# Shaping DMA transfers by their outermost size: eight-part loads and stores, uneven pieces, and a first result laid out by channel

## The chip, the cores and the metric

One core of a Trainium2 chip runs the whole program. The metric is the device time of one execution in microseconds (us). Runs of one kernel agree within about 1.2%; all timed runs quoted with a ratio were in the fast state. "Stages" below are read from one traced execution of each kernel: the **first stage** ends where the first `spread` matmul starts, **layer one** where the second set of them starts, **layer two** is the rest.

## The reference, cut to what matters

Two layers of the same form. Each normalises x over groups (32 groups along the last axis, statistics per sample over the other two axes), makes convolution weights for every position from a small network, and convolves:

```python
# x: (32, 32, 64, 256) = sample s, image b, channel c, position l, float32
w   = (relu(ln(z @ W1 + b1)) @ W2 + b2).reshape(B, L, CI, CO, 3)    # other weights at every position
out = einsum('sbilk,bliok->sbol', windows_of_3(gn(x)), w) + bias    # bias (B, CO, L) from another small net
x   = x + out                                                      # layer 0, then the same for layer 1
```

A "half sample" below is one image b and half its output channels, the unit `v` of the kernel's loop: 64 in each layer.

## The kernel before

The first stage loads all of x (64 MB) for statistics while it makes the hidden values and the bias, which it writes to DRAM (`hd`, `bd`). Then, for each half sample, TensorE makes the weights (`make`, into `pg`) and applies those of the previous half sample (`products`, into `pc`); DVE and ACT place the weights, DVE adds the products to the residual, GpSimd normalises x and adds the bias to the residual. All big transfers are issued on SP's queue.

```python
# layout in DRAM of x for statistics and residual, of x for layer one, of the first result, of the bias
xs: (128 = quarter of positions x sample, half sample, 32, 64)     xp: (image, 2, 128 = parity x channel, 16, 128)
x1 = [dram.tile([S, C, L], FP, name=f"x1_{b}") for b in range(B)]
bd = [dram.tile([2, NT, C, LT], FP, name=f"bd_{i}") for i in range(U // 2)]

def load_pairs(u, k):                      # x that is normalised
    t = pairs(u, k)
    if u < B:
        nc.sync.dma_start(out=t, in_=xp[u, k])
    else:
        src = x1[u - B][k * SH : (k + 1) * SH].rearrange("s c l -> c s l")
        nc.sync.dma_start(out=t[0:C], in_=src)
        nc.sync.dma_start(out=t[C:P, :, 0 : L - 1], in_=src[:, :, 1:L])

def load(q):                               # first statistics, 4 MB each, three in flight
    nc.sync.dma_start(out=xv[q % NX], in_=xs[:, q * SV : (q + 1) * SV])

def load_bias(v):                          # the same bias for all 32 samples
    ...
    for t in range(NT):
        src = bd[u // 2][u % 2, t, h * CH : (h + 1) * CH, :]
        nc.sync.dma_start(
            out=bts[v][t * S : (t + 1) * S],
            in_=bass.AP(src.tensor, src.offset, [[0, S]] + list(src.ap)),
        )
# ... (cut: normalisation, weights, products, stores)
```

Of the kernel before, what the change touches and what calls it, by code (L numbers as in the profile page):

```python
# [23 lines left out]
FP = mybir.dt.float32  # L24
# [6 lines left out]
P = 128  # L31
K = 3
G = 32
NT = 4
NH = 2
OG = 8
EPS = 1e-5
PARAMS = ("z", "W1", "b1", "g1", "be1", "W2", "b2", "Wb1", "bb1", "gb1", "beb1", "Wb2", "bb2")

# [2 lines left out]
def conv_layers(ctx: ExitStack, tc: tile.TileContext, xs: bass.AP, xp: bass.AP, layers: list, out: bass.AP):  # L42


    nc = tc.nc
    B, _, _, SH, M = xp.shape
    S, C, L = 2 * SH, P // 2, 2 * M
    A = layers[0]["z"].shape[0]
    E = L // G
    LT = L // NT  # L50
    MT = M // NT
    CH = C // NH
    EB = 512 // CH
    NB = LT // EB
    GT = G // NT
    F = 4 * CH
    WT = CH + MT * F + CH
    NL = len(layers)
    U = NL * B
    SV = 4  # L60
# [9 lines left out]
    dram = ctx.enter_context(tc.tile_pool(name="dram", bufs=1, space=DRAM))  # L70
    ps_g = ctx.enter_context(tc.tile_pool(name="ps_g", bufs=3, space=PSUM))
    ps_c = ctx.enter_context(tc.tile_pool(name="ps_c", bufs=2, space=PSUM))

    x1 = [dram.tile([S, C, L], FP, name=f"x1_{b}") for b in range(B)]
    hd = [dram.tile([2, P, L], FP, name=f"hd_{i}") for i in range(U // 2)]
    bd = [dram.tile([2, NT, C, LT], FP, name=f"bd_{i}") for i in range(U // 2)]

    w2 = big.tile([P, C, K * C], FP, name="w2t")

# [7 lines left out]
    rstd = const.tile([P, G, S], FP, name="rstd")  # L87
    parts = const.tile([P, GT, B, NH, 6], FP, name="parts")
    prep = const.tile([P, 3, GT], FP, name="prep")
    ident = const.tile([P, P], FP, name="ident")  # L90
# [3 lines left out]
    eps = const.tile([P, 1], FP, name="eps")  # L94
    nc.vector.memset(eps, EPS)

# [8 lines left out]
    for n, par in enumerate(layers):  # L105
        t = const.tile([P, K, C], FP, name=f"b2_{n}")
# [18 lines left out]
    def load_pairs(u, k):  # L125
        t = pairs(u, k)
        if u < B:
            nc.sync.dma_start(out=t, in_=xp[u, k])
        else:
            src = x1[u - B][k * SH : (k + 1) * SH].rearrange("s c l -> c s l")  # L130
            nc.sync.dma_start(out=t[0:C], in_=src)
            nc.sync.dma_start(out=t[C:P, :, 0 : L - 1], in_=src[:, :, 1:L])

    def residual(v):
        return ys[:, v % RING]

    def load_residual(v):
        u, h = divmod(v, NH)
        if u < B:
            nc.sync.dma_start(out=residual(v), in_=xs[:, v])  # L140
        else:
            for t in range(NT):
                nc.sync.dma_start(
                    out=residual(v)[t * S : (t + 1) * S],
                    in_=x1[u - B][:, h * CH : (h + 1) * CH, t * LT : (t + 1) * LT],
                )


# [20 lines left out]
    class Hidden:  # L169
# [54 lines left out]
        def bias(self):  # L224
            p3 = ps_c.tile([C, BLK], FP, tag="pc", name="p3")
            nc.tensor.matmul(p3, self.t["Wb2"], self.ht[:, 1, :], start=True, stop=True)  # L226
            bs = self.stage.tile([C, 2, M, 2], FP, tag="bs", name="bs", bufs=2)
            nc.scalar.activation(
                bs.rearrange("o b m a -> o b a m"),
                p3.rearrange("o (b a m) -> o b a m", b=2, a=2),  # L230
                AF.Identity,
                bias=self.t["bb2"],
            )
            nc.scalar.dma_start(
                out=bd[self.i].rearrange("b t o l -> o (b t) l"),
                in_=bs.rearrange("o b (t m) a -> o (b t) (m a)", t=NT),
            )



    def first_stats():

        NC = NH * B
        with tc.tile_pool(name="stage", bufs=1) as stage:
            spare = stage.tile([P, SV * CH * LT], FP, name="spare")
            flat = [xn.rearrange("p b m s -> p (b m s)"), spare, room]
            xv = [r[:, 0 : SV * CH * LT].rearrange("p (v o l) -> p v o l", v=SV, l=LT) for r in flat]
            NX = len(xv)

            def load(q):  # L250
                nc.sync.dma_start(out=xv[q % NX], in_=xs[:, q * SV : (q + 1) * SV])

            for q in range(NX):
                load(q)
                if q == 0:
                    small = [small_weights(stage, par, n) for n, par in enumerate(layers)]
            zts = []
            for j in range(2):
                zts.append(stage.tile([A + 1, ZB * BLK], FP, name=f"zt_{j}"))
                nc.vector.memset(zts[j], 1.0)  # L260

            made = {0: Hidden(stage, zts, small, 0)}

            def step(s, half):

                if half == 0:
                    if s in made:
                        made[s].project()
                    if s - 2 in made:
                        made.pop(s - 2).bias()  # L270
                    if s in made:
                        made[s].root()
                else:
                    if s - 1 in made:
                        made[s - 1].scale()
                    if s + 1 < U // 2:
                        made[s + 1] = Hidden(stage, zts, small, s + 1)

            n = NC * GT
            when = {k * n // (U + 4): k for k in range(U + 4)}  # L280
            for i in range(n):
                if i in when:
                    step(*divmod(when[i], 2))
                v, g = divmod(i, GT)
                u, h = divmod(v, NH)
                q, j = divmod(v, SV)
                nc.vector.bn_stats(parts[:, g, u, h, :], xv[q % NX][:, j, :, g * E : (g + 1) * E])  # L287
                if j == SV - 1 and g == GT - 1:
                    if q + NX < NC // SV:
                        load(q + NX)  # L290
                    if q + NX == NC // SV - 1:
                        for o0 in range(0, C, 2 * OG):
                            load_w2(0, o0, o0 + 2 * OG)
                    if q % NX == 2 and q + NX >= NC // SV:

                        for k in range(2):
                            load_pairs(0, k)
                        for v in range(2):
                            load_residual(v)

    def stats():

        st = parts.rearrange("p g b h (two f) -> p g (b h two) f", two=2)
        n = st.shape[2]
        shape = [P, GT, n]
        m, v, d = prep[:, 0], prep[:, 1], prep[:, 2]
# [25 lines left out]
    with tc.manual_schedule():  # L332
# [14 lines left out]
        bts = {}  # L347

        def load_bias(v):
            u, h = divmod(v, NH)  # L350
            bts[v] = bp.tile([P, CH, LT], FP, tag="bt", name="bt")
            for t in range(NT):
                src = bd[u // 2][u % 2, t, h * CH : (h + 1) * CH, :]
                nc.sync.dma_start(
                    out=bts[v][t * S : (t + 1) * S],
                    in_=bass.AP(src.tensor, src.offset, [[0, S]] + list(src.ap)),
                )

        def add_bias(v):
            y = residual(v)  # L360
# [2 lines left out]
        def store(v):  # L363
            u, h = divmod(v, NH)
            if u < B:
                for t in range(NT):
                    nc.sync.dma_start(
                        out=x1[u][:, h * CH : (h + 1) * CH, t * LT : (t + 1) * LT],
                        in_=residual(v)[t * S : (t + 1) * S],
                    )  # L370
            else:
                nc.sync.dma_start(out=out[:, v - NH * B], in_=residual(v))

        def normalize(u, k):
            ss = slice(k * SH, (k + 1) * SH)
# [7 lines left out]
        def make(h, kind, o0):  # L383
            pg = ps_g.tile([P, OG, M], FP, tag="pg", name="pg")
            even, odd = h[:, 0, :], h[:, 1, :]

            (k0, h0), (k1, h1) = (((1, even), (2, even)), ((0, odd), (1, odd)), ((2, odd), (0, even)))[kind]
            for k in range(OG):
                w = w2[:, o0 + k, :]
# [4 lines left out]
        def take(pg, n, kind, o0):  # L394

            def place(rows, a):
                a += o0 % CH
                return at(wall[rows, 0, a : a + 1], [[WT, NT], [F, MT], [1, OG]])

            def add(rows, a):  # L400
                nc.vector.tensor_tensor(  # L401
                    place(rows, a),
                    pg[rows].rearrange("p o (t m) -> p t m o", t=NT),
                    b2[n][rows, kind, None, None, o0 : o0 + OG].to_broadcast(
                        [rows.stop - rows.start, NT, MT, OG]
# [88 lines left out]
        for v in range(NH * U):  # L494
            u, h = divmod(v, NH)
# [32 lines left out]


def _orders(x):  # L530


    import numpy as np

    s, b, c, l = x.shape
    xs = x.reshape(s, b, NH, c // NH, NT, l // NT).transpose(4, 0, 1, 2, 3, 5)
    xp = x.reshape(2, s // 2, b, c, l // 2, 2).transpose(2, 0, 5, 3, 1, 4)
    return {
        "xs": np.ascontiguousarray(xs).reshape(P, b * NH, c // NH, l // NT),
        "xp": np.ascontiguousarray(xp).reshape(b, 2, P, s // 2, l // 2),  # L540
    }


# [23 lines left out]
def _result(y):  # L567
    import numpy as np

    y = y.reshape(NT, P // NT, -1, 64, y.shape[-1])  # L570
    return np.ascontiguousarray(y.transpose(1, 2, 3, 0, 4)).reshape(*y.shape[1:4], -1)


# [7 lines left out]
```

## Time and profile before

| kernel before | us |
|---|---|
| median of 4 runs | 4610.9 (4603.3 to 4617.2) |
| first stage, in the trace | 289.1 |
| layer one, in the trace | 2049.7 |
| layer two, in the trace | 2253.7 |

How to read it: the prediction works out that matmuls alone need 1928 us per layer, and that nearly all of the rest is "issue", time in which TensorE stands still and waits for nothing that the profile shows. The first stage is another matter: it is close to bound by the DMA engines. Its line in the busy times by stretch (start and end, length, then busy time of each engine with its count of instructions, granted clock, DMA share, GB/s):

```profile
200.00:250.00 50.00, 46.63 (x125) 28.02 (x124) 41.93 (x115) 22.56 (x35) 24.08 (x49) 0.57 0.85 309
```

The reader is to keep the last two numbers: DMA busy 0.85 of the time at 309 GB/s.

### The profile page before, as it was taken

What the parts mean: (1) busy time and instruction counts of PE and PEld (TensorE: products, weight loads), DVE (VectorE), ACT (ScalarE), POOL (GpSimd) and SP (SyncE); (2) the same over time, 40 slices, a digit from 0 to 9 for tenths busy, and PEclk for the clock granted to TensorE, in tenths of its full rate; (3) what the DMA queues carried; (4) which work ended last, traced back from release to release, by engine and by line L of the source; (5) the groups of instructions that cost most, each with busy time, mean ns of one, the idle gap of its engine ahead of it and who ended that gap; (6) DMA issues with size and microseconds to landing.
All of it is one profiled execution on the core that took longest, in us unless ns stands there. A gap on an engine that the chain in (4) does not pass through costs nothing.

```text
span 4592.5 us, 193878 instructions
## 1 busy us (share of the span) xinstructions
PE 4069.4 (89%) x90704; PEld 3883.6 (85%) x90704; DVE 2642.2 (58%) x3168; ACT 1291.2 (28%) x4264; POOL 2074.9 (45%) x618
## 2 busy tenths in 40 slices
PE   6889999999999999999969888888888888888888
PEld 3569999999999988899868888888888888888888
DVE  6876666666666666666645454545444554454455
ACT  3432232332322322223222222222222222222222
POOL 3465544455444554445344353353443533534532
PEclk9689999999999999999989999999999999999999
DMA  8874444445444454444567667576576675765764
GB/s 307 330 239 133 142 142 133 133 133 148 146 142 124 124 150 142 130 126 133 160 162 165 143 151 170 134 166 152 134 173 141 153 169 134 168 157 137 174 148 107
DMA packets 760621, 718.23 MB, mean 156 GB/s; under 512 B 567492, under 2 KB 715016, under 8 KB 716296
## 3 DMA queue, kind: packets, MB, share of 16 engines
q1 hardware_dynamic: 724488, 683.80, 56.5%
q10 hardware_dynamic: 35328, 22.03, 1.7%
q8 instruction: 709, 11.62, 1.1%
q14 instruction: 96, 0.79, 0.1%
HBM read 558.93 MB, written 146.80 MB: 154 GB/s over the span
## 4 chain that ended last, share of the span: by engine, by line
PE 82%; issue 9%; DVE 3%; DMA 3%; POOL 2%; ACT 1%; ACTq 0%; SPq 0%; POOLq 0%; DVEq 0%
PE pg L390 48%; PE pc L433 23%; PE pg L391 10%; DVE wall L401 2%; POOL sq L198 1%; DMA bd<-bs 1%; PE p L186 1%; DMA zt<-in_L_conv_z_dram 1%; DVE parts L445 1%; DVE room L442 1%; DMA room<-x 1%; PE p L226 0%; ACT ht L216 0%; ACT sq L190 0%; PE p L213 0%
## 5 line engine op out<-in xcount | busy, mean ns | idle before, releaser
L391 PE MATMUL pg<-hT,w2t 128*64 128x128 f32 x24576 | 2808.4, 278 | 60.7 <-issue 60.6
L390 PE MATMUL pg<-hT,w2t 128*64 128x128 f32 x24576 | 2808.6, 278 | 56.5 <-issue 48.2
L390 PEld LDWEIGHTS pg<-hT,w2t 128*64 128x64 f32 x24576 | 2758.8, 140 | 82.3 <-issue 61.9
L391 PEld LDWEIGHTS pg<-hT,w2t 128*64 128x64 f32 x24576 | 2759.2, 140 | 60.7 <-issue 60.7
L401 DVE TENSOR_TENSOR wall<-pg,b 128x1024 f32<-128x1024 f32 (+1 forms) x1536 | 1869.0, 1220 | 870.7 <-PE pg L391 866.8
L416 ACT ACTIVATE wall<-pg,b 64x128 f32<-64x128 f32 x4096 | 1176.7, 481 | 3090.3 <-DVE wall L401 2224.6
L380 POOL TENSOR_TENSOR xn<-room,gmean 128x2048 f32<-128x2048 f32 x128 | 606.6, 4739 | 2205.5 <-DMA room<-x 1104.4
L433 PE MATMUL pc<-wall,xn 128*32 128x128 f32 (+2 forms) x40960 | 1047.4, 261 | 313.3 <-issue 288.9
L433 PEld LDWEIGHTS pc<-wall,xn 128*32 128x32 f32 x40960 | 988.9, 114 | 379.1 <-issue 351.9
L442 DVE TENSOR_TENSOR room<-pc,room 128x512 f32<-128x512 f32 x512 | 354.1, 692 | 1002.4 <-PE pc L433 883.7
L380 POOL TENSOR_TENSOR xn<-xn,rstd 128x2048 f32<-128x2048 f32 x128 | 782.5, 6113 | 10.0
L361 POOL TENSOR_TENSOR room<-room,bt 128x2048 f32<-128x2048 f32 x128 | 593.4, 4636 | 82.3 <-DMA bt<-bd 72.3
L445 DVE BATCH_NORM_STATS2 parts<-room 128x6 f32<-128x256 f32 x512 | 192.9, 418 | 8.7
L198 POOL TENSOR_TENSOR sq<-sq 128x512 f32<-128x512 f32 (+2 forms) x192 | 103.6, 540 | 156.1 <-ACT sq L190 143.6
L186 PE MATMUL p<-wc,zt 17*128 17x256 f32 x256 | 99.8, 553 | 39.3 <-DMA zt<-in_L_conv_z_dram 39.3
L186 PEld LDWEIGHTS p<-wc,zt 17*128 17x128 f32 x256 | 67.5, 277 | 63.1 <-issue 39.7
L213 PEld LDWEIGHTS p<-ident,hs 128*128 128x128 f32 x256 | 50.2, 223 | 49.9 <-issue 49.9
L226 PE MATMUL p<-ht,Wb 128*64 128x512 f32 x64 | 56.7, 985 | 20.5 <-ACT ht L216 20.2
L213 PE MATMUL p<-ident,hs 128*128 128x128 f32 x256 | 62.7, 426 | 3.7 <-DVE hs L204 3.7
L287 DVE BATCH_NORM_STATS2 parts<-xn 128x6 f32<-128x256 f32 x192 | 64.0, 409 | 0.0
L287 DVE BATCH_NORM_STATS2 parts<-spare 128x6 f32<-128x256 f32 x160 | 53.5, 412 | 0.0
L287 DVE BATCH_NORM_STATS2 parts<-room 128x6 f32<-128x256 f32 x160 | 53.5, 412 | 0.0
(44 smaller groups left out, 231.4 us busy)
## 6 DMA issues: line engine op xcount, KB each, us to landing
bt<-bd SPq DMA_DIRECT2D x512, 256.0 KB, 8.9
room<-in_xp_dram SPq DMA_DIRECT2D x64, 1024.0 KB, 8.2
room<-in_xs_dram SPq DMA_DIRECT2D x64, 1024.0 KB, 6.4
x<-room SPq DMA_DIRECT2D x256, 256.0 KB, 4.2
room<-x SPq DMA_DIRECT2D x64, 1024.0 KB, 9.2
room<-x SPq DMA_DIRECT2D x256, 256.0 KB, 5.4
out_dram<-room SPq DMA_DIRECT2D x64, 1024.0 KB, 5.9
room<-x SPq DMA_DIRECT2D x64, 1020.0 KB, 12.9
```

The costliest lines, as they stand in the source:

```text
L186: nc.tensor.matmul(self.p1[:, k], self.zt[:, k * P : (k + 1) * P], self.t["wc"], start=True, stop=True)
L198: nc.gpsimd.tensor_tensor(to, self.sq[:, :, 0:w], self.sq[:, :, w : 2 * w], ALU.add)
L287: nc.vector.bn_stats(parts[:, g, u, h, :], xv[q % NX][:, j, :, g * E : (g + 1) * E])
L361: nc.gpsimd.tensor_tensor(y, y, bts.pop(v), ALU.add)
L380: nc.gpsimd.tensor_tensor(o, i, b, op)
L390: nc.tensor.matmul(pg[0:C, k, :], w[:, k0 * C : (k0 + 1) * C], h0, start=True, stop=True)
L391: nc.tensor.matmul(pg[C:P, k, :], w[:, k1 * C : (k1 + 1) * C], h1, start=True, stop=True)
L401: nc.vector.tensor_tensor(place(rows, a), pg[rows].rearrange("p o (t m) -> p t m o", t=NT), b2[n][rows, kind, None, None, o0 : o0 + OG].to ...
L416: nc.scalar.activation(place(rows, 0)[:, :, :, k], pg[rows, k].rearrange("p (t m) -> p t m", t=NT), AF.Identity, bias=b2[n][rows, kind, o0 ...
L433: nc.tensor.matmul(pc[t * S : (t + 1) * S, n0 - q * EB : n1 - q * EB, :], xn[:, u % 2, t * MT + p + 1, :], wall[:, t, a : a + (n1 - n0) * CH],
L442: nc.vector.tensor_tensor(part, pc.rearrange("p n o -> p o n"), part, ALU.add)
L445: nc.vector.bn_stats(parts[:, 2 * q + g, u, h, :], part[:, :, g * E : (g + 1) * E])
```

## The change

Its intent, as I read it: to confine the large transfers, by their number of outermost parts, to some of the 16 DMA engines and keep the others free. The data in DRAM are laid out again for that, and the first result by channel, so that a row of layer two's x is one run. The trace after has 8 packets of 8 KB open at a time in layer one (eight outermost parts) and 12 of 16 KB in layer two (36 and 24 parts), the one before 16 of 8 KB; "on 8 engines" and "on 12 engines" below stand for these numbers. The core of the diff (host layouts, comments and the inverse permutation of the result are cut):

```diff
-    x1 = [dram.tile([S, C, L], FP, name=f"x1_{b}") for b in range(B)]
+    x1 = [dram.tile([C, S, L], FP, name=f"x1_{b}") for b in range(B)]
-    bd = [dram.tile([2, NT, C, LT], FP, name=f"bd_{i}") for i in range(U // 2)]
+    bd = [dram.tile([2, NT, EIGHT // NT, C, LT], FP, name=f"bd_{i}") for i in range(U // 2)]
 # load_pairs
-            nc.sync.dma_start(out=t, in_=xp[u, k])
+            nc.sync.dma_start(out=t, in_=xp[:, 2 * u + k])
...
-            nc.sync.dma_start(out=t[0:C], in_=src)
-            nc.sync.dma_start(out=t[C:P, :, 0 : L - 1], in_=src[:, :, 1:L])
+        for c0, c1 in ((0, 36), (36, 60), (60, C)):
+            nc.sync.dma_start(out=t[c0:c1], in_=src[c0:c1])
+            nc.sync.dma_start(out=t[C + c0 : C + c1, 0 : SH * L - 1], in_=src[c0:c1, 1 : SH * L])
 # the bias is written twice
+            for r in range(EIGHT // NT):
+                nc.scalar.dma_start(out=bd[self.i][:, :, r].rearrange("b t o l -> o (b t) l"), in_=...)
 # first statistics
-                nc.sync.dma_start(out=xv[q % NX], in_=xs[:, q * SV : (q + 1) * SV])
+                for e in range(EIGHT):
+                    nc.sync.dma_start(
+                        out=xv[q % NX][e * PE : (e + 1) * PE].rearrange("p v o l -> p v (o l)"),
+                        in_=xs[e, q * SV : (q + 1) * SV].rearrange("v p o l -> p v (o l)"),
+                    )
 # load_bias: one transfer instead of four
+            src = bd[u // 2][u % 2, :, :, h * CH : (h + 1) * CH, :]
+            nc.sync.dma_start(
+                out=bts[v],
+                in_=bass.AP(src.tensor, src.offset, [[C * LT, EIGHT], [0, PE], [1, CH * LT]]),
+            )
 # result
-                nc.sync.dma_start(out=out[:, v - NH * B], in_=residual(v))
+                nc.sync.dma_start(out=out[:, v - NH * B].rearrange("e p o l -> e p (o l)"), in_=residual(v))
```

More of the change, by code (lines that the diff above doesn't have):

```diff
@@ L36 @@
 OG = 8
+EIGHT = 8
 EPS = 1e-5
@@ L45, in conv_layers @@
     nc = tc.nc
-    B, _, _, SH, M = xp.shape
+    B, _, SH, M = xp.shape[1] // 2, *xp.shape[2:]
     S, C, L = 2 * SH, P // 2, 2 * M
@@ L55, in conv_layers @@
     GT = G // NT
+    PE = P // EIGHT
     F = 4 * CH
@@ L127, in load_pairs @@
         if u < B:
-            nc.sync.dma_start(out=t, in_=xp[u, k])
-        else:
-            src = x1[u - B][k * SH : (k + 1) * SH].rearrange("s c l -> c s l")
-            nc.sync.dma_start(out=t[0:C], in_=src)
-            nc.sync.dma_start(out=t[C:P, :, 0 : L - 1], in_=src[:, :, 1:L])
+            nc.sync.dma_start(out=t, in_=xp[:, 2 * u + k])
+            return
+        src = x1[u - B][:, k * SH : (k + 1) * SH, :].rearrange("c s l -> c (s l)")
+        t = t.rearrange("p s l -> p (s l)")
+        for c0, c1 in ((0, 36), (36, 60), (60, C)):
+            nc.sync.dma_start(out=t[c0:c1], in_=src[c0:c1])
+            nc.sync.dma_start(out=t[C + c0 : C + c1, 0 : SH * L - 1], in_=src[c0:c1, 1 : SH * L])
     def residual(v):
@@ L139, in load_residual @@
         if u < B:
-            nc.sync.dma_start(out=residual(v), in_=xs[:, v])
+            nc.sync.dma_start(out=residual(v), in_=xs[:, v].rearrange("e p o l -> e p (o l)"))
         else:
@@ L144, in load_residual @@
                     out=residual(v)[t * S : (t + 1) * S],
-                    in_=x1[u - B][:, h * CH : (h + 1) * CH, t * LT : (t + 1) * LT],
+                    in_=x1[u - B][h * CH : (h + 1) * CH, :, t * LT : (t + 1) * LT].rearrange("o s l -> s o l"),
                 )
@@ L233, in bias @@
             )
-            nc.scalar.dma_start(
-                out=bd[self.i].rearrange("b t o l -> o (b t) l"),
-                in_=bs.rearrange("o b (t m) a -> o (b t) (m a)", t=NT),
-            )
+            for r in range(EIGHT // NT):
+                nc.scalar.dma_start(
+                    out=bd[self.i][:, :, r].rearrange("b t o l -> o (b t) l"),
+                    in_=bs.rearrange("o b (t m) a -> o (b t) (m a)", t=NT),
+                )
     def first_stats():
@@ L351, in load_bias @@
             bts[v] = bp.tile([P, CH, LT], FP, tag="bt", name="bt")
-            for t in range(NT):
-                src = bd[u // 2][u % 2, t, h * CH : (h + 1) * CH, :]
-                nc.sync.dma_start(
-                    out=bts[v][t * S : (t + 1) * S],
-                    in_=bass.AP(src.tensor, src.offset, [[0, S]] + list(src.ap)),
-                )
+            src = bd[u // 2][u % 2, :, :, h * CH : (h + 1) * CH, :]
+            nc.sync.dma_start(
+                out=bts[v],
+                in_=bass.AP(src.tensor, src.offset, [[C * LT, EIGHT], [0, PE], [1, CH * LT]]),
+            )
         def add_bias(v):
@@ L367, in store @@
                     nc.sync.dma_start(
-                        out=x1[u][:, h * CH : (h + 1) * CH, t * LT : (t + 1) * LT],
+                        out=x1[u][h * CH : (h + 1) * CH, :, t * LT : (t + 1) * LT].rearrange("o s l -> s o l"),
                         in_=residual(v)[t * S : (t + 1) * S],
@@ L371, in store @@
             else:
-                nc.sync.dma_start(out=out[:, v - NH * B], in_=residual(v))
+                nc.sync.dma_start(
+                    out=out[:, v - NH * B].rearrange("e p o l -> e p (o l)"), in_=residual(v)
+                )
         def normalize(u, k):
@@ L535, in _orders @@
     s, b, c, l = x.shape
-    xs = x.reshape(s, b, NH, c // NH, NT, l // NT).transpose(4, 0, 1, 2, 3, 5)
-    xp = x.reshape(2, s // 2, b, c, l // 2, 2).transpose(2, 0, 5, 3, 1, 4)
+    xs = x.reshape(2, s // 2, b, NH, c // NH, NT, l // NT).transpose(5, 0, 2, 3, 1, 4, 6)
+    xp = x.reshape(2, s // 2, b, EIGHT // 2, 2 * c // EIGHT, l // 2, 2).transpose(6, 3, 2, 0, 4, 1, 5)
     return {
-        "xs": np.ascontiguousarray(xs).reshape(P, b * NH, c // NH, l // NT),
-        "xp": np.ascontiguousarray(xp).reshape(b, 2, P, s // 2, l // 2),
+        "xs": np.ascontiguousarray(xs).reshape(EIGHT, b * NH, P // EIGHT, c // NH, l // NT),
+        "xp": np.ascontiguousarray(xp).reshape(EIGHT, b * 2, P // EIGHT, s // 2, l // 2),
     }
@@ L568, in _result @@
     import numpy as np
-    y = y.reshape(NT, P // NT, -1, 64, y.shape[-1])
-    return np.ascontiguousarray(y.transpose(1, 2, 3, 0, 4)).reshape(*y.shape[1:4], -1)
+    _, v, p, ch, lt = y.shape
+    y = y.reshape(NT, 2, v // NH, NH, p, ch, lt).transpose(1, 4, 2, 3, 5, 0, 6)
+    return np.ascontiguousarray(y).reshape(2 * p, v // NH, NH * ch, NT * lt)
 def kernel(**inputs):
```

## The prediction

> **What bounds the kernel now.** I read the page first: engines, queues, the chain.
>
> ```profile
> PE 4069.4 (89%) x90704; PEld 3883.6 (85%) x90704; DVE 2642.2 (58%) x3168; ACT 1291.2 (28%) x4264; POOL 2074.9 (45%) x618
> ...
> q8 instruction: 709, 11.62, 1.1%
> ...
> PE 82%; issue 9%; DVE 3%; DMA 3%; POOL 2%; ACT 1%; ACTq 0%; SPq 0%; POOLq 0%; DVEq 0%
> ...
> L390 PE MATMUL pg<-hT,w2t 128*64 128x128 f32 x24576 | 2808.6, 278 | 56.5 <-issue 48.2
> ...
> L433 PE MATMUL pc<-wall,xn 128*32 128x128 f32 (+2 forms) x40960 | 1047.4, 261 | 313.3 <-issue 288.9
> ```
>
> TensorE sets the time: 82% of the chain, and another 9% is "issue", TensorE standing still for nothing that the profile names. L390 and L391 run side by side, so a half sample (128 of them) costs (2808.6 + 1047.4) / 128 = 30.1 us of matmuls: 21.9 us making weights, 8.2 us of products. 64 of them are 1928 us per layer. The chain dates the layers: the statistics' `spread` matmuls begin at 289.13 and 2338.83 us. Layer one takes 2339 - 294 = 2045 us, 117 more than its matmuls; layer two from about 2388 (its first normalisation and load are over) to 4592, 2204 us, 276 more. The waits, first layer one (300 to 2338 us), then layer two (from 2400), account for these:
>
> ```profile
> PE pc L433 <- issue: 124.6, 56, 6.3
> ...
> PE pg L390 <- issue: 0.6, 1, 0.6
> ```
>
> ```profile
> PE pc L433 <- issue: 164.2, 101, 6.1
> ...
> PE pg L391 <- issue: 60.6, 24, 4.5
> ...
> PE pg L390 <- issue: 47.6, 17, 4.6
> ```
>
> 125 us and 272 us: nearly the whole excess of each layer, and none of it a wait for data. The queue lines say what it is. q8 moves 709 packets of 16 KB; 709 x 256 = 181,504 is TensorE's instruction count (2 x 90,704 = 181,408). So it fetches its own program, 256 instructions a packet. In products, 640 instructions in 8.2 us, a packet lasts 3.3 us; in the making of weights, 768 in 21.9 us, it lasts 7.3 us. I lined the q8 packets of the trace up with the instructions issued: the n-th fetch never starts before n + 0.7 packets of instructions have been issued, and TensorE stands still at n + 1.7 if it has not landed. So each fetch has the time of one packet, 3.3 or 7.3 us. A q8 packet takes 1.1 us once started, but it starts late: beyond that earliest moment by a median of 1.5 us in layer one (over 4 us in 53 of 353) and 2.1 us in layer two (over 4 us in 133 of 347, at worst 10.9 us). Late fetches fall where the data queue is full:
>
> ```profile
> 1000.00:1500.00 500.00, 468.50 (x11192) 458.45 (x11188) 320.82 (x383) 147.10 (x507) 242.24 (x48) 0.97 0.47 137
> ...
> 3500.00:4000.00 500.00, 430.70 (x9960) 418.94 (x9957) 244.30 (x226) 128.05 (x452) 215.04 (x43) 0.96 0.68 155
> ```
>
> In these windows the columns before the last are granted clock and DMA share: the clock is equal (0.97, 0.96), DMA 0.47 against 0.68, and TensorE loses 38 us in 500. DVE and GpSimd have slack; GpSimd's wait for x in layer two (1090 us) does not reach TensorE.
>
> [...] The trace does not name a packet's engine[...] the trace shows one block ahead and 397 us of stalls[...] an 8 KB packet takes 0.309 us in loads over 128 partitions but about 0.6 us in `bt` loads over 32, and a 1 KB packet 0.08 us in layer two's x (64 partitions) against 0.046 us in `hT` (128).
>
> **The change, part by part.** [...]
>
> Load per half sample and engine, from packet durations in the trace. Layer one before: residual 8 and x 8 packets x 0.309 = 4.9, `bt` 8 x 0.6 = 4.8, x1 store 256 x 0.016 = 4.1, sum 13.8 us of 32 (43%; the window says 0.47). [...] Layer two before: result 2.5, residual 256 x 0.018 = 4.6, x 128 x 0.08 = 10.2, `bt` 4.8, sum 22.1 us of 34.4 (64%; window 0.68). After, x1 lies by channel, so a row of x is one run of 16 KB instead of 16 of 1 KB: 10 to 12 rows x 0.62 us[...]
>
> [...] I leave a fifth of layer one's stalls (-100 us) and a quarter of layer two's (-205 us).
>
> Added: the first statistics read xs in eight transfers of 16 partitions instead of one of 128. [...] That stage is close to DMA-bound (share 0.83 to 0.90, 290 us). [...] 2048 x 1.36 / 16 = 174 us of packets of 32 KB now. [...] I book +40 us. The doubled `bd` stores (32 more transfers on ACT's queue) and the first x and residuals on 8 engines add +10. Transfer issues per half sample change little: `bt` 4 to 1, layer two's x 2 to 6, of 0.4 to 1 us each, on a queue that nobody but buffers waits for. The turn between the layers, where two x loads of 11.6 us lie on the chain, moves by under 5 us.
>
> Sum: 4610 - 100 - 205 + 40 + 10 = 4355 us.
>
> **Rivals.**
> 1. [...] Stalls of 397 us would grow by a third or more: about 4750 us.
> 2. *The eight engines become the bound.* [...] packets take 0.62 us, layer one has 48 x 0.62 + 4.1 = 33.9 us per half sample against 30.1 of matmuls, layer two as much. Then 128 x 33.9 + 340 = 4680 us or more. [...]
> 3. *The first statistics lose much more* (up to some +340 us with the slack now there) and eat the gain: about 4600 us.
> 4. [...] Layer one gains fully, layer two half: about 4450 us.
> 5. *Writes to x1 at steps of 32 KB instead of 1 KB are slower in HBM.* A store of 1 MB would take longer than its 4 to 5 us, but has half a sample of slack; under 30 us.
>
> **Range and chances.** Everything right with no loss ahead gives 4610 - 390, about 4220; the fourth rival, or a statistics stage longer by 200 us, gives 4450 to 4510; their mixtures reach 4600. I predict 4355 us, with 4210 to 4600 as the range. Rivals 1 and 2 together get 0.12, chiefly "slower"; the third gets most of 0.13 "same". Faster by over 2%: 0.75.
>
> **What would show it.** Right: "issue" before L433, L390 and L391 falls from 397 us to under 100, q8 packets start within about 1 us of their earliest moment in both layers, "issue" leaves the chain's first three, TensorE is at 0.94 or more in layer two, the first `spread` stays below 340 us. Wrong: 8 KB packets at 0.6 us rather than 0.309 (second rival), late q8 packets in layer one (first) or in layer two alone (fourth), DMA holding the chain before the first `spread` (third). If "issue" stays while q8 starts early, the stalls were not the fetch, and my main step falls.

## The result, and the profile after

The changed kernel takes 5151.6 us (median of 4 runs, 5130.3 to 5177.5) against 4610.9: ratio 1.118, 95% interval 1.112 to 1.123. Ratios here and below are the mean time of one kernel's fast runs over that of the other's fast runs of the same rounds, so not quite the ratio of the medians.

| stage, in the trace | before | after | difference |
|---|---|---|---|
| first stage | 289.1 | 718.2 | +429.1 |
| layer one | 2049.7 | 2097.9 | +48.2 |
| layer two | 2253.7 | 2312.5 | +58.8 |
| span | 4592.5 | 5128.6 | +536.1 |

Four fifths of the loss lie in a stage that the change was not meant for. From the page of the changed kernel, the lines that answer to those of before:

```profile
PE 4086.3 (80%) x90704; PEld 3893.3 (76%) x90704; DVE 2635.3 (51%) x3168; ACT 1292.0 (25%) x4264; POOL 2074.0 (40%) x618
...
q8 instruction: 709, 11.62, 1.0%
...
PE 55%; DMA 20%; issue 7%; DVE 6%; POOL 6%; SPq 4%; ACT 2%; ACTq 0%; DVEq 0%; POOLq 0%
...
L404 PE MATMUL pg<-hT,w2t 128*64 128x128 f32 x24576 | 2812.7, 277 | 115.3 <-issue 79.1
...
L447 PE MATMUL pc<-wall,xn 128*32 128x128 f32 (+2 forms) x40960 | 1050.6, 263 | 352.6 <-issue 233.6
```

The matmuls cost the same. In the chain, DMA has gone from 3% to 20%, and "issue", which should have left, is still there. Two stretches say where: the same one of the first stage as above, and one of layer two.

```profile
200.00:250.00 50.00, 16.24 (x38) 8.70 (x36) 13.21 (x36) 8.00 (x13) 10.29 (x21) 0.50 0.91 115
...
3500.00:4000.00 500.00, 423.22 (x9844) 413.35 (x9842) 240.96 (x224) 127.06 (x447) 213.87 (x42) 0.94 0.59 151
```

In the first stage the DMA engines are as busy as before (0.91) but move 115 GB/s instead of 309: packets of 8 KB took 1.08 us there on average, where those of 32 KB took 1.35 us before. DVE's waits of the first stage name the loads; before, it waited for none of them:

```profile
DVE parts L300 <- DMA xn<-in_xs_dram: 147.7, 5, 32.6
DVE parts L300 <- DMA room<-in_xs_dram: 115.8, 4, 30.6
DVE parts L300 <- DMA spare<-in_xs_dram: 114.4, 4, 32.1
```

TensorE's waits in layer one (718 to 2816 us), then in layer two:

```profile
PE pc L447 <- issue: 111.9, 62, 4.8
PE pg L404 <- DMA hT<-hd: 24.5, 1, 24.5
PE pg L404 <- issue: 19.5, 8, 4.3
```

```profile
PE pc L447 <- issue: 121.7, 62, 6.1
PE pc L447 <- DVE room L456: 101.8, 23, 20.3
PE pg L404 <- issue: 59.6, 24, 6.0
PE pg L405 <- issue: 47.6, 23, 4.7
```

With a further 7.6 us of L405, "issue" in layer one is 139 us (125 before), and one wait for the first hidden values comes on top. In layer two it is 229 us (272 before), but the wait for DVE's eviction (moving the products out of `pc`), 17 us before, is now 102 us. DVE waits there for GpSimd's bias addition:

```profile
DVE room L456 <- POOL room L373: 218.8, 29, 39.2
```

**Where the fetches run.** In the trace of after, 8 packets of 8 KB are open at a time in layer one (8.1 on average in busy stretches, against 16 before) and 12 of 16 KB in layer two: the shapes do narrow the transfers. The trace doesn't name a packet's engine, so it shows how many packets run at a time, not on which engines. I then took the lateness of each of TensorE's instruction fetches (its start minus the earliest moment, as in the prediction), grouped by which data packets were open at that moment, and by the number of the fetch modulo eight. Medians in us:

| fetch number mod 8 | 0 | 1 | 2 | 3 | 4 | 5 | 6 | 7 |
|---|---|---|---|---|---|---|---|---|
| before, layer one, beside 8 KB packets | 3.1 | 2.7 | 3.1 | 3.4 | 3.3 | 2.9 | 3.7 | 3.8 |
| after, layer one, 8 KB on 8 engines | 5.6 | 2.6 | 0.7 | 0.8 | 1.0 | 1.0 | 0.9 | 4.8 |
| after, layer two, 8 KB on 8 engines | 4.2 | 2.3 | 0.3 | 0.3 | 0.3 | 0.2 | 0.2 | 3.7 |
| after, layer two, 16 KB on 12 engines | 8.6 | 5.8 | 6.3 | 6.4 | 5.9 | 1.1 | 1.0 | 6.3 |

The lateness depends on the number modulo eight: beside the 8 KB packets of layer one after, number 0 is late by 5.6 us and number 2 by 0.7 us. I read this as fetches that go round eight places in turn, each with its own neighbours; a "place" below is such a number. With the data on 8 engines most places are prompt (0.2 to 1.0 us in both layers) and two or three late (2.3 to 5.6 us); in layer one two of them are later than any before (5.6 and 4.8 us against at most 3.8). (A number names a place within one kernel only: in stats_whole and all_eight, below, the late ones beside 8 KB packets in layer one are 6, 7 and 0, the same pattern one earlier.)

### The profile page after: what moved, and what is told of

The parts are those of the page before. It is cut to its first block, busy times and chain, and to the rows that moved or that the text cites. A ratio compares the mean times of both kernels' runs of the same rounds, so it can differ in the third digit from the quotient of the medians.

```text
span 5128.6 us, 193965 instructions
## 1 busy us (share of the span) xinstructions
PE 4086.3 (80%) x90704; PEld 3893.3 (76%) x90704; DVE 2635.3 (51%) x3168; ACT 1292.0 (25%) x4264; POOL 2074.0 (40%) x618
## 4 chain that ended last, share of the span: by engine, by line
PE 55%; DMA 20%; issue 7%; DVE 6%; POOL 6%; SPq 4%; ACT 2%; ACTq 0%; DVEq 0%; POOLq 0%
PE pg L404 32%; PE pc L447 15%; DMA bt<-bd 8%; PE pg L405 7%; DVE wall L415 3%; POOL xn L394 3%; DMA xn<-in_xs_dram 2%; POOL room L373 2%; DMA hT<-hd 2%; SPq L151 2%; DMA hd<-ht 2%; DMA bd<-bs 1%; DMA room<-in_xs_dram 1%; DMA room<-x 1%; PE p L194 1%
## 5 line engine op out<-in xcount | busy, mean ns | idle before, releaser
L405 PE MATMUL pg<-hT,w2t 128*64 128x128 f32 x24576 | 2812.7, 277 | 55.3 <-issue 55.1
L405 PEld LDWEIGHTS pg<-hT,w2t 128*64 128x64 f32 x24576 | 2754.1, 140 | 54.3 <-issue 54.0
L394 POOL TENSOR_TENSOR xn<-xn,rstd 128x2048 f32<-128x2048 f32 x128 | 778.3, 6080 | 10.0
L300 DVE BATCH_NORM_STATS2 parts<-room 128x6 f32<-128x256 f32 x160 | 53.6, 414 | 143.8 <-DMA room<-in_xs_dram 115.8
L224 ACT ACTIVATE ht<-p,be,g 128x512 f32<-128x512 f32 x32 | 24.5, 767 | 381.1 <-PE p L221 353.0
```

The lines of the kernel that those rows point to most:

```text
L300: nc.vector.bn_stats(parts[:, g, u, h, :], xv[q % NX][:, j, :, g * E : (g + 1) * E])
L394: nc.gpsimd.tensor_tensor(o, i, b, op)
L405: nc.tensor.matmul(pg[C:P, k, :], w[:, k1 * C : (k1 + 1) * C], h1, start=True, stop=True)
```

## The experiments

Fifteen kernels ran, all correct. Those of single parts start from the kernel before; `xf` in an edit is x in the order of before, handed over beside the new order where both are needed. For each timed kernel the median is given with that of the kernel before in the same rounds.

### The first stage: three kernels

**stats_whole**, the changed kernel with its first statistics undone:

```diff
-                for e in range(EIGHT):
-                    nc.sync.dma_start(out=xv[q % NX][e * PE : (e + 1) * PE]..., in_=xs[e, ...]...)
+                nc.sync.dma_start(out=xv[q % NX], in_=xf[:, q * SV : (q + 1) * SV])
```

> The changed kernel, with one thing undone: the first statistics read x again in one transfer of 128 partitions, from a copy of x in the order of before. Theory [...]: the first spread matmul starts at about 290 us instead of 718, the time falls by some 430 us to about 4720 us, still 2.3% slower than before, as layer one and layer two keep their 48 and 59 us. Rival (the long first stage comes from the doubled bias stores or from something else on the queues): the first spread stays above 600 us.

Measured: 4726.7 us (before 4619.9), ratio 1.025 (1.020 to 1.031). First stage 322.8 us, 33 us more than expected. Its traced execution took 4775 us, 1% above its other runs (4718 to 4728 us), so its layers (2114 and 2336 us) are not compared closely. The eighths are 718.2 - 322.8 = 395 of the 429 us; the remaining 34 us stay with the doubled bias stores and the first loads on 8 engines. (Below, bias_eight with the stores alone has 306 us, loads_eight with the loads alone 290 us, and only all_eight with both has 324 us.) The 2.5% that are left of the loss belong to these and to the two layers.

**stats_eighths**, the kernel before with that part alone:

```diff
-                nc.sync.dma_start(out=xv[q % NX], in_=xs[:, q * SV : (q + 1) * SV])
+                for e in range(EIGHT):
+                    rows = slice(e * PE, (e + 1) * PE)
+                    nc.sync.dma_start(out=xv[q % NX][rows], in_=xf[rows, q * SV : (q + 1) * SV])
```

> The kernel before, with one thing changed: each load of the first statistics is cut into eight transfers of 16 neighbouring partitions, in the order of x of before, so packets stay 32 KB. Theory [...] the first spread starts at about 720 us, the time is about 5040 us, the layers are unchanged. Rival (the 8 KB packets of the new order or the doubled bias stores are the cause): packets take about 1.3 us and the first spread stays at about 290 us, the time at 4610 us.

**stats_spread**, the same number of transfers, packets and bytes, other partitions:

```diff
+                    rows = slice(e, P, EIGHT)
```

> As the run with eighths, but each of the eight transfers has every eighth partition instead of 16 neighbours: as many transfers, packets and bytes[...]. Theory [...] the first spread starts at 380 to 430 us, the time is about 4720 us. Rival (the number of transfers or their small size is what costs): the same 720 us and 5040 us as the run with eighths.

Measured: eighths of neighbours 5000.9 us, first stage 673.7 us (720 expected); every eighth partition 4831.4 us, first stage 493.5 us (one run each, before 4619.9). The stretch from 200 to 250 us, first of neighbours, then of every eighth:

```profile
200.00:250.00 50.00, 15.05 (x36) 8.69 (x36) 13.21 (x36) 6.85 (x10) 6.86 (x14) 0.50 0.91 121
```

```profile
200.00:250.00 50.00, 22.11 (x59) 12.69 (x57) 22.94 (x64) 11.18 (x17) 10.29 (x21) 0.53 0.81 178
```

What decides is the mean time of the 2048 packets of 32 KB: 1.35 us from whole transfers, 2.42 us with every eighth partition, 4.24 us with 16 neighbours. By what mechanism the partitions of a transfer set the time of its packets, the traces do not show. The number of transfers is the same in the last two, so it is not what costs. Nor are packets of 8 KB or the order of x in DRAM: stats_eighths keeps those of before and loses 385 us (673.7 - 289.1), about what stats_whole won back (395). One part of the expectation missed: with every eighth partition the stage took 494 us, not 380 to 430. Packets account for 2048 x 2.42 / 16 = 310 us of it; why the rest is 184 us instead of 116 (289.1 - 2048 x 1.354 / 16 = 115.8) was not settled.

### Where TensorE's program is fetched: four kernels

Each adds copies from DRAM to DRAM to the kernel before, 12 per half sample, whose number of rows, 17 * k with k = 8, 12, 6 or 4, I chose so that each copy should spread evenly over k engines. That was my estimate and is not shown here; k serves as a name for the probes. They only probe; that they slow the kernel is of no interest.

```diff
+    NROWS, NW, NRING = 136, 512, 12          # 17 * k rows of 2 KB: 136, 204, 102, 68
+    quiet = [dram.tile([NROWS, 2 * NW], FP, name=f"quiet_{i}") for i in range(NRING)]
+    source = xf.rearrange("p v o l -> (p v) (o l)")[0:NROWS, 0:NW]
+    def stir():
+        nc.scalar.dma_start(out=quiet[spent[0] % NRING][:, 0:NW], in_=source)
 # after each take(...)
+                stir()
```

> The kernel before plus 12 copies per half sample, in HBM, of 136 rows of 2 KB[...]. The trace of the changed kernel suggests that TensorE's fetches go round eight places in turn: beside transfers of 8 engines numbers 7, 0 and 1 of each eight are late and 2 to 6 are not. Theory [...]: in layer one the mean lateness of fetches 7, 0, 1 of each eight rises by 2 us or more above that of fetches 2 to 6. Rival (one engine fetches everything, and the pattern of eight is an accident of this kernel's phases): all eight rise alike, or none.

> As the run with copies[...], but 204 rows[...]. Theory: fetches 7, 0, 1, 2, 3 and 4 of each eight are late, 5 and 6 are not. Rival (one engine): all alike.

> As the run with copies[...], but 102 rows[...]. [...] fetches 7 and 0 of each eight were late (4.6 and 3.9 us median beside copies, against 0.7 to 1.3 us of the others)[...]. Theory [...]: no fetch is late, all medians within 1 us of each other, issue waits in layer one near 125 us. Rival [...]: 7 and 0, or one of them, late by 3 us or more.

> The same with 68 rows [...] Theory: no fetch is late; the time rises only by what the copies cost the data transfers. Rival: late ones as with 8.

Measured: 6606, 6989, 6446 and 6080 us (one run each, before 4614 to 4620). Median lateness in us of fetches in layer one that fell due beside copies (11 to 34 fetches in each cell; the first two rows leave out fetches beside which 8 KB packets were open too, the last two keep them):

| rows of a copy | 0 | 1 | 2 | 3 | 4 | 5 | 6 | 7 |
|---|---|---|---|---|---|---|---|---|
| 68 (k = 4) | 0.2 | 0.3 | 0.2 | 0.3 | 0.2 | 0.4 | 0.4 | 0.2 |
| 102 (k = 6) | 0.8 | 0.3 | 0.4 | 0.5 | 0.5 | 0.6 | 0.3 | 3.2 |
| 136 (k = 8) | 4.6 | 1.3 | 0.8 | 0.7 | 0.7 | 1.0 | 0.7 | 3.9 |
| 204 (k = 12) | 5.6 | 4.6 | 3.6 | 3.9 | 1.2 | 0.8 | 1.0 | 4.7 |

No place is late at k = 4 (at most 0.4 us), one at k = 6 (number 7), one more at k = 8 (number 0), three more at k = 12 (1, 2 and 3). The other three stay at 0.2 to 1.2 us in all four. On which engines the places lie was not shown. Counted like the last two, the first two rows read 0.8 to 1.4 us, and 0.6 to 1.1 us with 3.6 us for number 7, which says the same. The single-engine rival falls: it had all eight alike, and at k = 8 they read 0.7 to 4.6 us. The theories missed in parts: for k = 8 number 1 was to be late and is hardly so (1.3 us), for k = 12 number 4 was to be late and is not, for k = 6 none was to be late and one is; that for k = 4 held. The raised numbers next to a late place (1 beside 0) may be lateness handed on, since fetches come in order: none of the 709 overlaps another in the traces of before and after. Number 4 stays open: late beside the 12-engine pieces of the changed kernel (5.9 us), not here (1.2 us).

### The parts of the change in the two layers: five kernels

**x1_channel**, the first result by channel, layer two's x in whole transfers:

```diff
-    x1 = [dram.tile([S, C, L] ...
+    x1 = [dram.tile([C, S, L] ...
+        nc.sync.dma_start(out=t[0:C], in_=src)                       # rows of 16 KB
+        nc.sync.dma_start(out=t[C:P, 0 : SH * L - 1], in_=src[:, 1 : SH * L])
```

> The kernel before, with one thing changed: the first result lies by channel, sample, position; layer two reads its x in whole transfers of 64 channels[...]. Theory: rows of 16 KB instead of 16 rows of 1 KB[...]; layer one unchanged within 15 us, layer two 0 to 60 us shorter; 4550 to 4620 us. Rival (stores at steps of 32 KB are slow in HBM and cause layer one's 48 us): layer one longer by 40 us or more, 256 B packets above 0.016 us.

Measured: 4626.2 us (before 4619.9), ratio 1.002 (0.999 to 1.004). Layer one 2048 us, with 256 B packets at 0.016 us as before: stores at steps of 32 KB cost nothing. Layer two 2282 us. Packets of 16 KB took 1.20 to 1.23 us, 8 of them 9.7 us per half sample and engine (10.2 before): longer rows do not help here. In the other kernels here that leave layer two as it was, its traces read 2262 to 2269 us, so about half of the 28 us may be scatter.

**all_eight**, only layer one's x, residual, bias and result in eight parts (the bias stored twice, as in the change):

```diff
+            nc.sync.dma_start(out=t, in_=xp[:, 2 * u + k])                       # layer one's x
+            nc.sync.dma_start(out=residual(v), in_=xs[:, v].rearrange("e p o l -> e p (o l)"))
+            nc.sync.dma_start(out=bts[v], in_=bass.AP(..., [[C * LT, EIGHT], [0, PE], [1, CH * LT]]))
+                nc.sync.dma_start(out=out[:, v - NH * B].rearrange("e p o l -> e p (o l)"), in_=residual(v))
```

> The kernel before with the eight-part shapes of layer one's x, the residual, the bias and the result alone: first statistics in whole transfers, first result by sample, second-layer x in whole transfers. Theory (three of the eight fetch places stay beside a load of twice the length, so nothing is won): TensorE's issue waits in layer one 110 to 150 us as before (125), layer one 2050 to 2115 us; layer two 2254 to 2330 us with new waits for the bias; the first stage 290 to 325 us because of the doubled bias stores; 4600 to 4740 us in all. Rival (the shapes are harmless or good, and only the statistics and the pieces cost): issue waits below 80 us in layer one and a total below 4560 us.

Measured: 4739.2 us (before 4614.2), ratio 1.028 (1.024 to 1.031); first stage 324 us, layer one 2106 us, layer two 2308 us. The stages came as expected. TensorE's "issue" waits in layer one were 162 us, above the expected 110 to 150 and the 125 of before, and those of layer two 300 us against 272. New waits for the bias in layer two did not come: the wait for DVE's eviction was 17 us as before, so the 102 us of the changed kernel need its other parts too.

**loads_eight**, layer one's x and residual alone in eight parts, the bias still in four transfers:

```diff
+            nc.sync.dma_start(out=t, in_=xp[:, 2 * u + k])
+            nc.sync.dma_start(out=residual(v), in_=xs[:, v].rearrange("e p o l -> e p (o l)"))
```

> The kernel before with the eight-part shape of layer one's x and residual alone; bias, result, statistics and first result as before. Theory: layer two within 15 us of before (2254), layer one 2030 to 2090 us (before 2050)[...]; 4590 to 4650 us. Rival (eight engines bound layer one): layer one above 2110 us.

Measured: 4981.4 us (before 4614.2), ratio 1.080 (1.076 to 1.085); layer one 2426 us, layer two 2262 us. The rival's threshold was passed, but not by its mechanism alone, since all_eight has more loads in eight parts and is faster (4739 us). TensorE's waits in layer one (290 to 2716 us):

```profile
PE pc L436 <- issue: 383.8, 77, 10.0
```

In this kernel 32% of the 8 KB packets of layer one took over 0.7 us, against 4% before and 4% in all_eight; 84% of these slow ones ran while 14 or more packets were open, that is with the bias in its four whole transfers beside x in eight parts. Fetches 0 and 7 were late by 8 us there, the others by 2 to 5 us. So beside this mixture every place is late. Transfers of different shape alone do not: in bias_four and bias_eight (below), where whole loads of x and residual are issued before the bias in four or eight parts, 4% and 5% of the packets took over 0.7 us. Whether it is the order, or the four bias transfers of 32 partitions each, was not tested.

**x1_pieces**, x1_channel with layer two's x in pieces of 36, 24 and 4 channels, the bias in four transfers:

```diff
+        for c0, c1 in ((0, 36), (36, 60), (60, 64)):
+            nc.sync.dma_start(out=t[c0:c1], in_=src[c0:c1])
+            nc.sync.dma_start(out=t[C + c0 : C + c1, 0 : SH * L - 1], in_=src[c0:c1, 1 : SH * L])
```

> The kernel before with the first result by channel and layer two's x in pieces of 36, 24 and 4 channels; all other transfers as before. Against the run with whole transfers by channel (layer two 2282 us). Theory (5 or 6 of eight fetch places stay beside x[...]): layer two 2270 to 2350 us, no gain. Rival [...]: layer two below 2250 us and issue waits in layer two below 220 us.

Measured: 4872.4 us (before 4619.6), ratio 1.054 (1.051 to 1.058); layer one 2052 us, layer two 2536 us, worse than expected. In layer two (from 2346 us):

```profile
PE pc L439 <- DVE room L448: 295.3, 41, 20.0
PE pc L439 <- issue: 138.2, 47, 7.9
PE pg L396 <- issue: 48.9, 15, 5.5
PE pg L397 <- issue: 40.6, 17, 4.6
```

"Issue" did fall to 228 us (291 in x1_channel), as the pieces were meant to do, and the eviction wait of 295 us (16 in x1_channel) is the price. GpSimd's waits in that layer say what came late:

```profile
POOL xn L386 <- DMA bt<-bd: 603.9, 39, 29.5
POOL room L367 <- DMA bt<-bd: 497.0, 26, 26.3
POOL xn L386 <- DMA room<-x: 218.8, 20, 19.3
```

It is the bias: 1101 us, against 35 us in x1_channel, while its wait for x fell from 1132 us. So the pieces win 63 us of fetch stalls and lose more. TensorE's wait is the one of the changed kernel, but what lies behind it is not: there, with the bias in one transfer, GpSimd waits 35 us for the bias and 1202 us for x.

**bias_eight**, the bias alone in eight outermost parts, with its doubled stores:

```diff
+            nc.sync.dma_start(out=bts[v], in_=bass.AP(..., [[C * LT, EIGHT], [0, PE], [1, CH * LT]]))
```

> The twin of the run with four outermost parts: the bias load alone in eight outermost parts [...], with the doubled bias stores that this needs; all else as before. Theory [...]: the first stage 320 to 325 us; fetches 7 and 0 of each eight, or two neighbours, are late in layer one beside 8 KB packets, the others early; issue waits in layer one 90 to 150 us against 45 with four; total 4600 to 4680 us. Rival [...]: layer one below 1970 us as with four, total 4500 to 4560 us.

Measured: 4567.0 us (before 4619.2), ratio 0.989 (0.987 to 0.992). First stage 306 us, layer one 2000 us, layer two 2255 us. This part alone is a gain of 1.1%, under the 2% from which the record calls a run faster; the total and the first stage were better than expected, and "issue" in layer one (97 us) lies where the theory had it, between the 45 us of four parts (below) and the 125 us of before. Late in layer one beside 8 KB packets: fetches 0 and 7 (4.6 and 3.0 us), the others 1.2 to 2.1. The rival (that the gain of four parts comes from one transfer instead of four) asked for layer one below 1970 us, so it doesn't explain the gain of four parts alone; but it may have the 28 us of "issue" that fell here too.

### Four parts instead of eight: three kernels

**bias_four**. The four quarters of positions are four outermost parts already, so nothing has to be stored twice:

```diff
-            for t in range(NT): ...            # four transfers of 32 partitions
+            src = bd[u // 2][u % 2, :, h * CH : (h + 1) * CH, :]
+            nc.sync.dma_start(
+                out=bts[v],
+                in_=bass.AP(src.tensor, src.offset, [[C * LT, NT], [0, S], [1, CH * LT]]),
+            )
```

> The kernel before with the bias load in one transfer of four outermost parts [...] instead of four of 32 partitions on 16 engines. [...] Theory [...]: no gain, layer one 2050 to 2200 us, total 4600 to 4900 us. Rival (fetches beside less data win): issue waits under 90 us in layer one, total under 4560 us.

Measured: 4505.4 us (before 4619.6), ratio 0.975 (0.972 to 0.977). My theory fell, the rival stands: layer one 1936 us instead of 2050, no fetch place later than the others (1.3 to 1.9 us in all eight, 2.7 to 3.8 before), and 8 of 353 late by over 4 us instead of 53. TensorE's waits in layer one, then the stretch from 1000 us, to be laid beside the one in the prediction:

```profile
PE pc L435 <- issue: 45.0, 45, 6.0
```

```profile
1000.00:1500.00 500.00, 487.67 (x11916) 475.75 (x11914) 341.09 (x407) 157.54 (x542) 255.45 (x50) 1.00 0.46 145
```

"Issue" falls from 125 to 45 us. The DMA share is the same (0.46 and 0.47); what has changed is the shape of one load. The granted clock is 1.00 instead of 0.97. TensorE's idle time in layer one falls from 147 to 76 us, and the other 43 of the 114 us won are shorter busy time. The clock records of the trace have 29 stretches at half clock in layer one before, 133 us in all; shortly before each of them (within 4 us) TensorE had stood still for 2.0 to 5.2 us in one piece. In bias_four there are 3, 31 us in all. No run here varied the length of a stall alone.

**bias_four_l1** does this in layer one only:

```diff
+            if u < B:
+                (the one transfer)
+                return
             for t in range(NT): ...
```

> The bias load with four outermost parts in layer one, and as before in layer two, where four parts gave 2278 us against 2254. Theory [...]: layer one about 1936 us, layer two about 2254 us, total 4470 to 4495 us, 0.5% below the run with four in both. Rival (layer two's 25 us is scatter): no faster than 4505 us.

Measured: **4496.3 us** (before 4619.2), ratio 0.973 (0.971 to 0.975), the fastest version of this study. Layer one 1934 us, layer two 2269 us. Its interval and that of bias_four overlap, so the rival (layer two's difference is scatter) is not excluded.

**four_out** gives the result store four outermost parts too:

```diff
-                nc.sync.dma_start(out=out[:, v - NH * B], in_=residual(v))
+                nc.sync.dma_start(out=out[:, v - NH * B].rearrange("t p o l -> t p (o l)"), in_=residual(v))
```

> As the run with four outermost parts of the bias in layer one, and the result stored with four outermost parts too. Theory [...]: layer two within 30 us of 2254 either way; total 4460 to 4520 us. Rival (fetches win clearly): layer two below 2200 us. Rival (the engines bound): above 2300 us.

Measured: 4597.2 us (before 4619.2), ratio 0.996 (0.994 to 0.999). Layer one 1935 us, layer two 2386 us (its traced execution was the slowest of six, 20 us above the median). The theory (within 30 us of 2254, total up to 4520) missed, and the threshold of the second rival, engines as the bound, was passed. Giving a transfer four parts is not good in itself: here, beside layer two's x (1 KB packets), fetches were late by 8.2 to 9.8 us instead of 5.7 to 7.8 in bias_four_l1, and "issue" in layer two rose from 285 to 354 us. Why the result in four parts makes the fetches beside x later was not tested.

## Why the prediction was wrong, by its own steps

The prediction was 4355 us; the kernel took 5152.

- **What bounds the kernel: right.** The stalls called "issue" are late instruction fetches: one load in four outermost parts took 80 of 125 us of them (28 of these came with eight parts too) and left 8 of 353 fetches late by over 4 us instead of 53, and lateness follows the probes from step to step of k (no place late, then one, two and five).
- **"The first x and residuals on 8 engines": right** in number: 8 packets are open. Layer two's pieces of x have 12.
- **"-100 us" and "-205 us" for the stalls: the step that failed first.** The sum and rivals 1 and 4 took the fetch to run on one engine; that was an estimate, which the trace before could not test. The trace after has a pattern of eight, with two or three places late beside data on 8 engines (2.3 to 5.6 us) and six beside data on 12 (5.8 to 8.6 us). "Issue" went from 125 to 139 us and from 272 to 229 us: rival 1 has the direction of layer one, rival 4 that of layer two. As fetches come in order, two late places of eight are enough to stop TensorE.
- **"I book +40 us" for the first statistics: the step that failed most.** The +40 was an estimate with no measured packet behind it. The trace after has a mean of 1.08 us for a packet of 8 KB over the stage, and medians of 0.9 to 1.2 us in the stretches of 2 us that I looked at. With the measured packet the sum would have been 8192 x 1.08 / 16 = 553 us instead of 174, +379; the eighths alone cost 395 us by undoing them. This was rival 3, whose "+340 us" was too small as well.
- **"Doubled bd stores and first loads on 8 engines +10": mis-sized.** What was left of the first stage's loss after the eighths is 34 us; 17 us of it came in bias_eight, which has the doubled stores but not the loads, and 1 us in loads_eight, which has the loads alone.
- **Rival 2, "the eight engines become the bound": half.** Packets took 0.50 us on average in layer one, between 0.309 and the 0.62 us of the rival; layer one came to 2098 us, where the 33.9 us per half sample of the rival would make 64 x 33.9 = 2170.
- **"10 to 12 rows x 0.62 us": mis-sized.** A row of 16 KB took 1.15 us in the changed kernel, so on 12 engines x costs each about 128 x 1.15 / 12 = 12 us per half sample, not the 6 to 7 of the product, and no less than before (10.2).
- **Layer two:** the pieces brought a wait that no step had, DVE's eviction behind the bias addition, 102 us. That the pieces cause it is shown by x1_pieces against x1_channel (295 and 16 us), and in the surroundings of the change by stats_whole against all_eight, which differ in the result by channel and the pieces alone: 120 and 17 us, with "issue" at 254 and 300 us. The single parts measured alone (all_eight +54, x1_channel +28, x1_pieces +282 us in layer two) do not add up to the 59 us of all together. The record shows where they part: x1_pieces alone has GpSimd wait 1101 us for the bias, and the one bias transfer of the change doesn't. Whether its eight parts or its being one transfer does that stays open.
- **Rival 5, "writes at steps of 32 KB are slower": wrong**, 0.016 us a packet as before.
- **The idea behind the change was sound, its boundary was not.** One and the same load gains 2.5% in four outermost parts, 1.1% in eight with the copies that eight parts need, and x, residual and result on top of it turn the gain into a loss.

## What to carry to other kernels

When a tensor engine waits for "issue" and the kernel is long and unrolled, line the instruction packets up with the data packets before looking at data waits: the program itself is a DMA stream (here 709 packets of 16 KB, with 397 us of TensorE standing still for late ones), and the shape of a transfer changed how many of its packets run at a time (16, 12 or 8 here). Give one load at a time fewer outermost parts and measure, since more of the same (x, residual, result) lost what the first move won. And never cut a large load into groups of neighbouring partitions without measuring its packets: here the same bytes in as many packets took 1.35 us each from whole transfers, 2.42 us with every eighth partition and 4.24 us with 16 neighbours.
